# A three-block transformer step on one core: residual and bias adds moved from identity matmuls to VectorE, and a new instruction order

## The chip, the cores and the metric

The kernel runs on one core of a Trainium2 chip. The core has five engines, each with an instruction stream of its own: TensorE (PE) multiplies matrices and writes to PSUM, its weight loads are shown as PEld; VectorE (DVE) works elementwise and reduces along rows; ScalarE (ACT) evaluates functions and copies; GpSimd (POOL) does some small work; SyncE (SP) issues the loads and stores. The streams wait for each other by semaphores only. The metric is the device time of one launch in microseconds (us), the median of several runs. Before the change it is 224.31 us, the median of 3 runs between 224.06 and 224.98.

## The reference

Two rows (batch 2) of 128 tokens with 512 channels go through three residual blocks, each on a layer norm of the row. Everything is float32.

```python
x = x + xattn(layernorm(x), ctx, ...)   # causal self-attention, cross-attention to 2048 context tokens, MLP
x = x + rwkv(layernorm(x), ...)         # the "time" axis is the batch: 2 steps
x = x + moe_attn(layernorm(x), ...)     # attention with expert-mixed values and outputs

# in xattn (single head of 512 channels, scale 1/sqrt(32)):
z = self_attn(x, Wq1, Wk1, Wv1);  x = layer_norm(x + z, ln1_g, ln1_b)
z = cross_attn(x, ctx, Wq2, Wk2, Wv2);  x = layer_norm(x + z, ln2_g, ln2_b)
z = relu(x @ fc1_w + fc1_b) @ fc2_w + fc2_b;  out = layer_norm(x + z, ln3_g, ln3_b)

# end of rwkv:
h = layernorm(inp + (y * g) @ Wo, norm_w, norm_b)
out = layernorm(silu(h @ Wf + bf), lnf_w, lnf_b)

# end of moe_attn: 8 heads of 64, 5 experts, of which 2 are chosen by logits
out = einsum('bthe,bthk,ekd->btd', mask_o, attn, Wo)
```

The self-attention's key count is found from the scores themselves (number of scores of the first query that are not zero), as is that of the cross-attention.

## The kernel before

A row of tokens is a 128 x 512 tile: a token to a partition, the channels along it. Both rows go through the same phases: `queries` (layer norm and Q, K, V of both rows), `self_attention`, `cross_queries`, `cross_attention`, `feed_forward`, `rwkv`, `switch_heads`. For a projection the row is turned (four 128x128 transposes by PE, `turn`) and multiplied with the weights by `project`, mostly in two halves of 256 output channels, each in its own PSUM bank. `matmuls` lists the products of one bank. Where it is given `plus`, it puts one more product in front, the identity `unit` with the row that is to be added: PE adds a residual or a bias into the bank by a matmul.

To be fast, part of the large operands are split into a high and a low half in a reduced float32 format (tiles named hl_; high by an ACT cast, low by a VectorE subtraction) and multiplied in three products; the rest are plain float32 products, which leave two records per matmul in the profile.

The steps of importance here:

- `self_attention` (from line 554): scores, `count`, softmax, the transposed probabilities `pT`, then per half of 256 channels the residual `h` by identity matmul and `pT` times V in the same bank (line 578), moments by `bn_stats` from the bank, and the normalised `x1`.
- `rwkv` (from line 778): after gating, `Y` is turned into `yT`, multiplied with Wo with the residual `inp` as `plus` (line 959), normalised into `hh`, turned, and multiplied with Wf with the bias row `par2[BF]` as `plus` (line 982). ACT takes the tanh of the bank, VectorE forms `f` from tanh and bank.
- `switch_heads` (from line 999): at the end VectorE multiplies the attention output `po` of the even and the odd heads (`par` 0 and 1) with the expert mask into two tiles `me[0]` and `me[1]`. In row 1 the sum over the 8 heads and the transposition are done at once by PE: for each of three pairs of experts eight matmuls with `unit` are summed in a bank (lines 1106 to 1110), four from each tile. Row 0 sums on VectorE and transposes.

The order of work is not that of the program text. Every operation is only recorded (`Program`, `Engine`), and `emit` (line 166) issues the records in the sequence of the string `ORDER`, in which a number is a record and "+2" stands for the two records after it. The sequence is fixed and sets the order on every engine and in the load queue, all by line 169, so all instructions have that line in the profile. Pools give buffers in the order of the records: `stage` (3 buffers of 128 x 512) takes the quarters of weights that are split, `wide` (16) the whole weights, context tiles, rows of parameters and large intermediates. A load waits until the earlier user of its buffer is done, and the loads behind it in the queue wait with it. Eight PSUM banks rotate likewise. `keep_warm` puts a few idle identity matmuls into the stream; `NDUM` and `TAILW` say how many.

Of the kernel before, what the change touches and what calls it, by code (L numbers as in the profile page):

```python
# [42 lines left out]
0 208 1 209+1 215 2 1698 216+1 1718 218 1719 219+1 1699 232 221 1700 8 4 211 3 212 233 222 25 234 20 235+1 214 213 238  # L43
237 228 223+1 26 239 229 21+1 31 244+1 225 246 1720 270 240 247 27 230+1 241 271+3 248 275+2 249 28 34 37 226 23+1
278+1 250+5 280 242 227 256 281 257 243 258+2 282+1 261+3 284+1 265+1 286 29 292 30 32 293+1 287+2 267 35 318 33 295+2
319+1 38 298 36 299+1 321 39 301 322 302+2 323+4 305 328+1 306+1 330+1 5 308+1 332 310+4 333+2 315 40+1 49 43+1 11 19
336 9 337+2 290 268+1 317 340+1 344+1 414 316 415 45 42 346+1 375 12 50 79 46+1 84 376 66 48 291 343 358+1 342 360 377
361 416 51 362 378 348 363 18 379 417 364 87 67 63 418 104 380 419 349 381 365 384 382 56 420 423 350+4 395 366 383
385+1 85 387+2 421+1 424 390 425 69 426 391 6 355 367+1 392 357 396 356 427 393 428 369 429 68 434 371 370 372 397 394
398+3 430 402 373 431+1 435 404+1 433 57 403 436+2 406 1721 407+3 1701 453 463 411 454 10 80 439 455 464 456 465 457  # L50
441 443 466 440 442 447 467 444 468 82 458+2 448 469 74 445 86 88 446 473 483 474 470 450 449 475+2 484+2 478+2 58 64
60+1 471 81 461 481 487+2 493 94 59 62 89 494 490 495+1 462 482 521+2 497 491 65 75 472 524 492 498 525+2 499 528 500
529 109 83 530 501+4 531 97 126 532 374 506 533 77 76 534 507+6 535+1 95 514+2 537+2 98 540 517 541+1 588+1 562 96 518
543+1 563 72 575 564 576 545 78 519 590+2 577 593 565+6 594 578 546 579 70 73 572 549 573 580+1 550 582+1 71 551+2 105
584+1 99 547 106 520 548 92+1 554 586 555+1 595 90 727 596 557 91 558+2 597+1 728 157 599 107 729 102 100 574 108 587
121 127 561 730+2 600 112 733+1 129 735 601+3 101 736+1 618 740+5 738 605 611 606 612 609 746+1 753 748+1 610 607+1
613 54 766+1 754+1 750+1 768+1 615 614 756+2 641 770 623+3 642 771 122 759 103 760 55 643 761 772 616 627 128 773+1
762 775+2 130 644 739 628 123 629 617 630+4 124 635 125 645 137 136 138 763+1 646 752 765 928 636 659 778 660+2 637
140 638+2 779 131 142 663+1 780 647+4 132+1 652+2 781 113+1 134 782 655+1 796 168 657+1 665+1 677 667 135 668 785 783
678 669+2 679 672 787 680 13 15 110 786 784 673+2 789 681 790 676 682+1 619 684 788 791 145 197 792 17 14 794 52 837+2  # L60
7 840 801+1 795 855 803 53 169 139 793 804+1 685 819+1 807 821 856 822 808 857 141 16 111 146 806 809+2 686 812+1 118
143 687 823 814 688 815 689 816+1 692 818 144 825+1 693 824 827+1 858 147 158+1 690 696 829 697 691 830 698+1 831 700
832+2 701 835 841+1 412 115+1 694 702 119 703 413 120 695 117 704+1 150 620 152 706 836 148+1 621 187 622 859 188 151
843+1 707 710 708 711 709 712 845+3 713 163+1 178 849+1 179 714 797 715 451 851+1 165 189 853+1 860+1 716 720+1 153
862 717 723 722 718 180 719 863 904 864 725 905+1 916 866 917 867 907+2 452 865 870+1 868 874 910 875+2 911 170 981
724 869 872 878 154 879 155 880+2 918 160 166 873 883+2 919 161 920+1 913 912 156 914 726 922+1 929+1 798+2 175 931
176 924 167 932 925 162 926 915 933 172 888 886 934+2 889 887 890+2 937 177 938 184 927 893 939+1 894+1 898 199 943
941 896+1 944 942 899+1 969 957 901 173 970 945 958+4 185 963+1 946 966 947+1 971+1 951 949 952 965 950 953+1 973+2
967 955 976+1 956 982 968 983+2 193 902 978 986 1010 987 1011 979 988 1013+1 989+1 1012 991 980 992 1015 1089 1016 993
1017 1099 174 186 181 903 994 1090 996 1020 1067 1022 1069 1108 1018 1107 997 995 998 1091 1024 1140 1092 1073 1109  # L70
1026 1071 1141+1 1139 1028 1100 1029 1075 1093+1 1076 198 1077 1095 1030+1 1101 1070 1021 190 1096 1023 1032 1078 999
182 1033 1102 1116+1 1068 1079 1034 1080 191 196 1001 1004 1000 1025 1005 1035 1002 1006 1003 1007 183 1008 1103 1027
1009 1036 171 1072 1218+1 1081 1037 1221 194 1038 1082 1220 1222 1224+1 1039 1223 1097 195 192 1111 1110 1228 1324
1083 1112+2 1118 1323 1327 1119 1226 1229 1325 1333 1328 1084 1334+1 1326 1085 1336 1045 1329 1040 1074 1086 1343 1231
1279 1098 1282 1307 1346 1330 1280 1308 1232 1281 1233 1283 1046 1305 1344 1230 1234 1044 1306 1115 1047 1284 1286+2
1042+1 1104 1285 1019 1289 1337 1290 1347 1291+1 1235 1293+1 1120 1105 1087 1041 1048 1352 1295 1088 1296 1345 1391
1353 1297 1354+1 1348 1148+1 1392 200 1054 1389 1349+1 1106 1390 1050+1 1309 1150+1 201 1052 1331 1049 1121 1123 1236
1055 1061 1338 1124 1393 1299 1298 1300 1053 1060 1125 1310 1332 1311+1 1237 1122 1356 1339 1127 1238+3 1131 1242+1
1058 1244+1 1301 1341 1059 1246+2 1143 1340 1056 1062 1132 1351 1144 1128 1064 1342 1133 1063 1065 1302 1129 1357 1130
1303 1399 1145+1 1135 1057 1126 1313 1066 1314 1152 1359 1315 1253 1136 1254 1360 1137 1376 1358 1400 1316+3 1256 1252  # L80
1249 204 1250 1170 1401 1134 1251 1255 1138 1153 1257 1264 1258+1 1377 1261 1154 1361 1265 1155 1304 1147 1156 1158+1
1263 1320 1157 1161+1 1164 202 1369 1262 1260 1268 1321 1160 1165 1171 1166 1163 1167 1172 1168 1363 1378 1173+1 1276
1402 1198 1190 1394 1322 1277 1395 207 1373 1278 1379 1273 1267 1270 1269 1374 1380 1382 1362 1272 1371 1375 1274 1169
1396 1364 1271 203 1366 1275 1175 1381 1176 1383 1177 1384 1372 1385+2 1365 1178 1367+1 1388 1180 1179 1370 1266
1181+2 1397 1184 1186 1185 1187+1 1199+2 1189 1202 1191+1 205 1193+1 1403 1398 1203 1404 1406 1405 1407+2 1204 1410+1
1205 1424 1415 1195 1412+2 1416 1418 1417 1419+2 1196+1 1206+3 1212 206 1210 1213 1211 1214+3 1473 1425 1452 1426+2
1422 1472 1475+1 1444 1474 1423 1478+1 1429+2 1477 1481 1480 1432 1487 1482 1434 1433 1436 1435 1227 1437 1483 1440+1
1484 1438+1 1442 1488 1445 1485 1446 1489 1522 1453+2 1523 1447 1443 1513 1456 1448 1511 1486 1457 1524+1 1505 1526+1
1514+1 1490 1516 1496+1 1491+1 1517 1528 1518 1529 1493+1 1498 1519 1499 1520 1506+4 1500 1449 1521 1495 1530 1501
1512 1531 1502+2 1559 1534 1458 1450 1459 1451 1460+3 1466 1464 1467 1465 1468+2 1533 1471 1560+2 1602 1601 1603 1532  # L90
1604 1607+1 1563 1605 1539+2 1606 1567 1542 1564 1536 1610 1609 1543 1565 1611 1566 1535 1612+1 1569 1545 1544 1547
1546 1570 1552 1642 1549 1643 1572+1 1550 1614 1571 1551 1651 1553+1 1652 1537+1 1653 1555 1575 1556 1576 1574 1577
1548 1616 1654 1557+1 1617 1635 1634 1636+1 1568 1644+1 1618+1 1578 1646+1 1620+1 1648 1615 1625 1655 1622 1656 1623
1649 1638 1657 1640 1582 1650 1658 1624 1626+4 1639 1631 1659 1632 1688+1 1633 1579 1641 1663+1 1580 1583 1581 1690+1
1584 1660 1585 1662 1668+2 1586 1692 1671 1696 1587 1661 1588+1 1695 1672 1590 1705 1676 1706 1596 1591 1597 1673+1
1678 1675 1681 1679 1682 1665 1694 1592 1666 1693 1702 1667 1703 1680 1684+1 1683 1686 1677 1712 1687 1707 1697 1704
1708 1713 1709+2 1714 1716+1 1715 1598 1593 1731+1 1722 1733 1740+1 1734 1594 1599 1735 1600 1742 1723+4 1736+1 1743
1728+1 1738 1744+1 1730 1749 1746 1739 1747+1 1595 1754 1750+3 1755+3
"""
OPT = set("""psc fc2 Wv Wk u2col bfpe z4pe z1pe q2 hhcol q2row d3 both1 both4""".split())  # L100

ON_ACT = [set("vsum vc vv bv".split()), set("vsum vc vv bv".split())]
PCR = [{0,1,2},{0,1,2}]
WHOLE = set("Wv1 Wv2 fc2 Wv Wk".split())
VPE = set()
MIX = {"Wq1": 2}
MIXD = set("Ww Wa Wr".split())
CUTW = 2
# [77 lines left out]
def perceiver_kernel(ctx: ExitStack, tc: tile.TileContext, a: dict, out: bass.AP):  # L186
# [46 lines left out]
    for t in range(T):  # L233
        for j in range(2):
            sync.dma_start(X[t][:, half(j)], a["x"][t][:, half(j)])
# [296 lines left out]
    def token(t):  # L532
        return slice(t * P, (t + 1) * P)
# [678 lines left out]
```

## Time and profile before

| | us |
|---|---|
| median of 3 runs | 224.31 (224.06 to 224.98) |
| the profiled execution | 224.74 |
| its span, from first to last instruction | 222.9 |
| PE busy | 215.3, 1246 records |
| VectorE busy | 186.1, 439 records |
| ScalarE busy | 140.2, 400 records |
| GpSimd busy | 17.1, 40 records |
| loads | 43 MB, 195 GB/s on average |
| granted TensorE clock | 0.998 of full speed |

The page cuts the span into 40 slices and gives the busy share of each engine in tenths for every slice. Its chain follows the work that ended last back from the end: at each step to what released the instruction, or to the instruction before it on its engine. A group line gives the shape, the count, then busy time and mean duration, then the idle time of the engine just before such instructions and what ended it. Records of matmuls overlap (a matmul's end is modelled), so that the busy time of PE is no proof that it runs at its peak.

### The profile page before, as it was taken

The numbers are of one execution on the slowest core, as the hardware profiler recorded it, in microseconds if no ns is written. First come the engines' busy times: TensorE is split into PE (matmuls) and PEld (weight loads), VectorE is DVE, ScalarE is ACT, GpSimd is POOL, SyncE is SP. The second block draws the span as 40 slices with busy tenths as digits, with TensorE's granted clock in tenths as the row PEclk, the third lists the DMA queues.
The fourth block names the chain that finished last, engine by engine and source line by source line (L and its number), as shares of the span: only waits on it lengthen the run. The fifth ranks groups of instructions, "written<-read, shape, count | busy, mean of one in ns | idle before, by whom it ended". The sixth has DMA issues, their size and how long they took to land.

```text
span 222.9 us, 3686 instructions
## 1 busy us (share of the span) xinstructions
PE 215.3 (97%) x1246; PEld 182.7 (82%) x1246; DVE 186.1 (83%) x439; ACT 140.2 (63%) x400; POOL 17.1 (8%) x40
## 2 busy tenths in 40 slices
PE   6999999999999999999999999999999999998993
PEld 6999879998778767868788888887886799797892
DVE  4670569998999998989989999999998598999831
ACT  2753569686788998827469889977652614705500
POOL 4200011000000000000111100021213001000000
PEclk9999999999999999999999999999999999999999
DMA  6987799926699999587854999900000000000011
GB/s 157 355 322 255 250 381 386 385 110 238 245 315 354 374 399 375 202 285 209 310 187 102 402 389 387 303 7 0 3 0 0 0 3 1 0 3 0 0 50 47
DMA packets 21897, 43.42 MB, mean 195 GB/s; under 512 B 1283, under 2 KB 2871, under 8 KB 21879
## 3 DMA queue, kind: packets, MB, share of 16 engines
q1 hardware_dynamic: 21879, 43.19, 55.1%
q8 instruction: 10, 0.16, 0.3%
q14 instruction: 8, 0.07, 0.1%
HBM read 42.66 MB, written 0.52 MB: 194 GB/s over the span
## 4 chain that ended last, share of the span: by engine, by line
PE 64%; DVE 24%; DMA 3%; issue 2%; POOL 2%; ACT 2%; SPq 0%; POOLq 0%; DVEq 0%
PE bank L169 64%; DMA w_Wv<-in_Wv_dram 3%; DVE me L169 2%; DVE hl_ctxT L169 2%; DVE Y L169 2%; DVE pr L169 2%; DVE st L169 1%; DVE em L169 1%; DVE hl_ctxN L169 1%; POOL rinv L169 1%; POOL rs L169 1%; DVE ve L169 1%; DVE v L169 1%; DVE u L169 1%; DVE hl_Wv L169 1%
## 5 line engine op out<-in xcount | busy, mean ns | idle before, releaser
L169 POOL TENSOR_TENSOR rinv<-ve,nhalf 128x1 f32<-128x1 f32 x16 | 10.1, 629 | 147.2 <-DVE ve L169 75.4
L169 DVE TENSOR_TENSOR hl_ctxT<-cT,hl_ctxT 128x1024 fp32r<-128x1024 f32 x16 | 19.0, 1216 | 0.8 <-ACT hl_ctxT L169 0.5
L169 PE MATMUL bank<-hl_ctxT,qkTh 128*128 128x512 f32 x64 | 17.8, 395 | 0.1
L169 ACT CAST hl_ctxT<-cT 128x1024 fp32r<-128x1024 f32 x16 | 16.0, 1050 | 2.5 <-PE bank L169 2.5
L169 PE MATMUL bank<-hl_ctxN,pTh 128*128 128x512 f32 x48 | 16.3, 402 | 0.0
L169 DVE TENSOR_TENSOR hl_ctxN<-cN,hl_ctxN 128x1024 fp32r<-128x1024 f32 x12 | 14.4, 1217 | 0.6 <-ACT hl_ctxN L169 0.6
L169 PEld LDWEIGHTS bank<-hl_ctxT,qkTh 128*128 128x128 f32 x64 | 11.7, 188 | 2.8 <-DVE some L169 0.5
L169 DVE TENSOR_TENSOR hl_Wv<-w_Wv,hl_Wv 128x512 fp32r<-128x512 f32 x12 | 8.0, 681 | 6.4 <-ACT hl_Wv L169 6.4
L169 ACT CAST hl_ctxN<-cN 128x1024 fp32r<-128x1024 f32 x12 | 12.3, 1046 | 0.0
L169 PE MATMUL bank<-hl_ctxT,qkTl 128*128 128x512 f32 x32 | 10.4, 396 | 0.0
L169 PEld LDWEIGHTS bank<-hl_ctxN,pTh 128*128 128x128 f32 x48 | 8.9, 189 | 1.6
L169 PE MATMUL bank<-xnT,w_fWk 128*128 128x128 f32 x64 | 10.2, 276 | 0.0
L169 PE MATMUL bank<-hl_ctxN,pTl 128*128 128x512 f32 x24 | 10.1, 421 | 0.0
L169 ACT CAST hl_Wv<-w_Wv 128x512 fp32r<-128x512 f32 x12 | 7.3, 622 | 4.0 <-DMA w_Wv<-in_Wv_dram 3.9
L169 PE MATMUL bank<-xnT,w_fWq 128*128 128x128 f32 x64 | 9.9, 277 | 0.0
L169 PEld LDWEIGHTS bank<-u2T,w_fc 128*128 128x128 f32 x64 | 8.2, 191 | 1.4 <-ACT u2T L169 1.1
L169 PEld LDWEIGHTS bank<-xnT,w_fWq 128*128 128x128 f32 x64 | 8.6, 192 | 0.7 <-ACT xnT L169 0.3
L169 PEld LDWEIGHTS bank<-xnT,w_fWk 128*128 128x128 f32 x64 | 8.9, 192 | 0.2
L169 PE MATMUL bank<-u2T,w_fc 128*128 128x128 f32 x64 | 8.5, 278 | 0.3 <-ACT u2T L169 0.3
L169 PE MATMUL bank<-w_Wa,mix 128*128 128x256 f32 x32 | 8.7, 379 | 0.0
L169 PE MATMUL bank<-unit 128*128 128x128 f32 x32 | 6.9, 391 | 1.7 <-POOL unit masks.py:199 1.7
L169 PE MATMUL bank<-w_Wr,mix 128*128 128x256 f32 x32 | 8.4, 379 | 0.0
(289 smaller groups left out, 614.8 us busy)
## 6 DMA issues: line engine op xcount, KB each, us to landing
cT<-in_ctxT_dram SPq DMA_DIRECT2D x8, 1024.0 KB, 6.7
cN<-in_ctx_dram SPq DMA_DIRECT2D x8, 1024.0 KB, 7.5
spread<-in_spread_dram SPq DMA_DIRECT2D x9, 512.0 KB, 8.5
w_Wv<-in_Wv_dram SPq DMA_DIRECT2D x12, 256.0 KB, 5.3
w_Wk<-in_Wk_dram SPq DMA_DIRECT2D x8, 256.0 KB, 5.3
w_Wq<-in_Wq_dram SPq DMA_DIRECT2D x4, 256.0 KB, 4.5
w_Wk2T<-in_Wk2T_dram SPq DMA_DIRECT2D x4, 256.0 KB, 6.9
w_Wq<-in_Wq_dram SPq DMA_DIRECT2D x1, 1024.0 KB
```

The source lines that it names most:

```text
L169: self.tc.keep_in_program_order(op(*args, **kwargs))
```

## The change

Four things are done by VectorE that PE did by identity matmuls, and the order is new.

- First attention, both rows (`z1d`): no `plus`; VectorE adds `h` to the bank into the half of `x1`, and moments and normalisation read `x1` instead of the bank.
- Wo, both rows (`Z4D`): no `plus`; VectorE adds `inp` to the bank into the half of `hh`, and moments and normalisation read `hh`.
- Wf, row 1 only (`BFD`): the path without `plus`, which was in the code: VectorE adds the bias into `f`, ACT takes the tanh of `f`, VectorE forms the product from `f`.
- Head sums, row 1 (`me2`): before the matmuls of a pair of experts VectorE adds the pair of `me[1]` onto that of `me[0]`, and PE sums four products instead of eight.
- `ORDER` is another sequence throughout, for the loads too.

The options `xact`, `u1back` and `pow1` come into the text but are not switched on.

```diff
-0 208 1 209+1 215 2 1698 216+1 1718 218 1719 219+1 1699 232 221 1700 8 4 211 3 212 233 222 25 234 20 235+1 214 213 238
...
+215+3 0 208 1718+1 219+2 1 209+1 1720+1 222 2 232 211 3 21 233 4 234+1 20 212 236 213 22 214 223+1 228 225 229 237
...
-OPT = set("""psc fc2 Wv Wk u2col bfpe z4pe z1pe q2 hhcol q2row d3 both1 both4""".split())
+OPT = set("""psc me2 z1d fc2 Wv Wk u2col bfpe z4pe z1pe q2 hhcol q2row d3 both1 both4""".split())
...
+Z4D, BFD = {0, 1}, {1}
...
             for j in range(2):
                 pz = bank([P, C // 2])
-                matmuls(pz, [(pT[:, :P], V[t][:, half(j)])], True, h[t][:, half(j)])
-                dve.bn_stats(m.st[:, j, :], pz)
-                zs.append(pz)
+                if "z1d" in OPT:
+                    matmuls(pz, [(pT[:, :P], V[t][:, half(j)])], True)
+                    z = x1[:, half(j)]
+                    dve.tensor_add(z, pz, h[t][:, half(j)])
+                else:
...
+                dve.bn_stats(m.st[:, j, :], z)
+                zs.append(z)
...
+        hh = row("hh")
         m = Moments()
         if "z4pe" in OPT:
             zs = []
-            for j, c, po in project(yT, W["Wo"], plus=inp):
+            for j, c, po in project(yT, W["Wo"], plus=None if t in Z4D else inp):
+                if t in Z4D:
+                    zz = hh[:, c]
+                    dve.tensor_add(zz, po, inp[:, c])
+                    po = zz
                 dve.bn_stats(m.st[:, j, :], po)
                 zs.append(po)
...
-        if "bfpe" in OPT:
+        if "bfpe" in OPT and t not in BFD:
             for j, c, po in project(hhT, W["Wf"], plus=par2[BF]):
...
             for c, e in enumerate((0, 2, 3)):
                 pt = bank([P, P])
                 keep_warm(0 if c else TAILW[2], pt)
-                matmuls(pt, [(m[:, i, e : e + 2, :].rearrange("p e d -> p (e d)"), unit) for m in me for i in range(4)], True)
+                if "me2" in OPT:
+                    n = pairs[c]
+                    dve.tensor_add(me[0][:, :, n], me[0][:, :, n], me[1][:, :, n])
+                ms = me[:1] if "me2" in OPT else me
+                matmuls(pt, [(m[:, i, e : e + 2, :].rearrange("p e d -> p (e d)"), unit) for m in ms for i in range(4)], True)
                 act.copy(aT[:, c, :], pt)
```

## The prediction

> **What bounds the kernel now.** The page first: engine shares, slices, chain.
>
> ```profile
> span 222.9 us, 3686 instructions
> ...
> PE 215.3 (97%) x1246; PEld 182.7 (82%) x1246; DVE 186.1 (83%) x439; ACT 140.2 (63%) x400; POOL 17.1 (8%) x40
> ...
> PE   6999999999999999999999999999999999998993
> ...
> DVE  4670569998999998989989999999998598999831
> ...
> PE 64%; DVE 24%; DMA 3%; issue 2%; POOL 2%; ACT 2%; SPq 0%; POOLq 0%; DVEq 0%
> ```
>
> TensorE (PE) is busy nearly everywhere, but VectorE (DVE) is close behind from a sixth of the span on. So an engine's share over the span settles nothing; I cut the span where the chain that ended last changes its engine, and asked for busy time in these stretches.
>
> ```profile
> 18.00:33.11 15.11, 15.11 (x88) 12.60 (x88) 7.01 (x31) 8.75 (x23) 0.64 (x2) 1.00 0.85 307
> 33.11:41.45 8.34, 8.34 (x75) 8.27 (x74) 7.93 (x17) 6.46 (x13) 0.87 (x7) 1.00 1.05 385
> 41.45:112.94 71.49, 70.36 (x356) 55.56 (x355) 67.08 (x131) 53.12 (x94) 1.49 (x2) 1.00 0.83 291
> 112.94:143.60 30.66, 30.66 (x157) 26.45 (x158) 29.78 (x82) 27.24 (x99) 2.35 (x4) 1.00 0.84 296
> 143.60:172.08 28.48, 27.85 (x131) 22.86 (x129) 26.92 (x79) 17.43 (x85) 5.91 (x6) 1.00 0.03 11
> 172.08:192.89 20.81, 20.81 (x128) 16.95 (x129) 16.86 (x42) 10.16 (x36) 2.07 (x3) 1.00 0.00 1
> 192.89:204.64 11.75, 11.75 (x107) 11.44 (x105) 11.41 (x22) 3.34 (x11) 0.00 (x0) 1.00 0.01 1
> ...
> 209.67:219.89 10.22, 9.77 (x72) 8.88 (x71) 4.70 (x9) 0.76 (x3) 0.00 (x0) 1.00 0.08 27
> ```
>
> After length come PE, PEld, DVE, ACT, POOL, then clock, DMA share, GB/s. VectorE has room in the first attention (7.01 of 15.11) and in the tail (4.70 of 10.22). Between 33.11 and 172.08 it has 131.7 of 139.0 us: two engines are full at once, and in 143.6 to 172.1 the chain runs over VectorE (pr, Y, st, f, X, xn, one behind the other) while PE is at 98%. The prices come from the groups by shape and from the timeline:
>
> ```profile
> L169 PE MATMUL bank<-unit,me 128*128 128x128 f32 x48 | 5.7, 276 | 0.0
> ...
> L169 PE MATMUL bank<-h,unit 128*128 128x256 f32 x8 | 2.5, 392 | 0.0
> L169 PE MATMUL bank<-inp,unit 128*128 128x256 f32 x8 | 2.4, 380 | 0.0
> L169 PE MATMUL bank<-spread,unit 128*128 128x256 f32 x8 | 2.2, 379 | 0.0
> ```
>
> ```profile
> 151.35 1.89 PE L169 MATMUL bank<-w_Ww,mix 128*128 128x256 f32 x8
> 211.29 5.11 PE L169 MATMUL bank<-unit,me 128*128 128x128 f32 x44
> 212.88 0.75 DVE L169 TENSOR_TENSOR res<-bank,X 128x256 f32<-128x256 f32 x2
> ```
>
> **The change, part by part.** A float32 matmul leaves two records that overlap their neighbours, so the mean of one is no price. Eight records of 128x256 take 1.89 us: (1.89 - 0.38)/7 = 0.216 a record, 0.43 us a matmul. For 128x128, (5.11 - 0.28)/43 = 0.112, 0.225 us a matmul. Gone are four h,unit, four inp,unit, two of the four spread,unit and twelve of the 24 unit,me matmuls: 10 x 0.43 + 12 x 0.225 = 7.0 us of PE. New on VectorE: ten adds of 128x256 (0.42 each, 0.33 where another follows: 0.75 - 0.42), two of 128x512 (0.69 or 0.60, from the ve products, 1.29 for two) and one more of 256: 10 x 0.33 + 2 x 0.60 + 0.33 = 4.8 us. ACT's count stays at 342 instructions. The edits and the order work together, so I go by stretch.
>
> *First attention (18 to 33).* PE sheds 4 x 0.43 = 1.7, but the chain scores, count, exp, V matmul, moments, x1 then has no filler left. Before, the last score of row 0 is followed by its count at 24.55, 3.85 after the first Wv1 matmul at 20.70; the new order puts six Wv1 matmuls (0.23) and five scores (0.225) there, 2.5 us, so the chain starts 1.35 earlier. It grows by two adds in front of the moments, 0.7. I take -0.65; PE waits about 1 us in that chain. Bounds: -1.7 (PE full) and +0.7 (the start gains nothing). Row 1's chain has row 0's Wq2 matmuls as cover; without it, its own two adds would cost 0.7, within the bound. The scheme needs the second cT load sooner: SyncE now issues two cT before the fourth Wv1 quarter, which waits for a stage buffer anyway (issued 14.88 before).
>
> *The middle (33 to 172).* From the two instruction orders, with a duration for each from the trace: VectorE's work from the first x1 to row 0's xn was 130.3 us and is 128.6. Two low halves of ctxT (1.2 each) move ahead of the softmax of the first attention, into idle time; row 0's two Wo adds (0.7) and the bias add into row 1's X (0.6) come in front of xn; the rest are shifts. PE loses four Wo identities and one Wf identity there, 5 x 0.43 = 2.15. At the share it has now (0.948), VectorE needs 128.6/0.948 = 135.7, 1.8 less by its own count. Both engines allow about the same: -1.9. Bounds: -2.15, and +1.3, if the early ctxT halves buy nothing (0.7 + 0.6 stay).
>
> *Loads.* ACT's casts of Wv quarters waited 3.9 us for DMA, and the chain has 6.95 us of that load just before 108.9; PE then waits 0.3 at 110 and 0.3 at 113. The new SyncE order issues one Wv quarter among the cT loads, all eight cN in a row and fc1 at PE's 77th us of work instead of at 95.1 us. I take the two waits as gone: -0.6; bounds 0 and -1.2, twice that, for the waits that ride on them. Wg, Wo and Wf move behind fcat, fWk and fWq: by buffer releases they leave at about 120, 125 and 136 and are used at 147, 156 and 161. With 2.5 MB ahead at 300 GB/s (8 us) they still land first; without that cover a late Wf costs what it is late. POOL's order changes by nothing on the chain.
>
> *Row 1 after 172.* PE loses 0.43 (the other Wf identity). Row 1's chain gets two Wo adds (0.7, during PE's fcat and fWq of row 0) and two Wf adds in front of the tanh, 0.42 not covered, since the q/k matmuls left behind Wf last 5.4 + 1.6 and the chain there took 7.1. Tanh sits behind these adds on ACT with only evacuations queued after it. Net 0, bounds -0.4 and +0.7. The 192.9 to 204.6 stretch is VectorE's, 11.41 of 11.75, with the same instructions in slightly other order: 0, bounds -0.6 and +0.6 (one ve product).
>
> *Tail.* From the first me product of row 1 (209.67) PE ends 9.8 us later. Now: product 1.40, product of the first pair 0.69, its add 0.69 and a hand-over 0.1: PE starts the pair's four matmuls at +2.9 instead of +1.6. Pair two and three follow VectorE (0.6 + 0.6, then 0.4 + 0.45): the last four matmuls begin at +5.05 and end at +5.95; six fWo matmuls of 0.43 make +8.55. Gain 1.2, where PE alone would give 2.7. Bounds -2.7 and +0.3 (three adds uncovered, 1.8, less half of 2.7 with waits).
>
> Sum: -0.65 - 1.9 - 0.6 + 0 - 1.2 = -4.35. Against the profiled execution, 224.74 (span 222.9 and 1.8 around it), 220.4; this execution stood 0.4 over the median of 224.31, so **220.0**.
>
> [...]
>
> **Rivals.**
>
> (1) PE alone binds. For it: its waits for others sum to only 4.0 us. Against: the chain in 143 to 172. All 7.0 come back: 217.3.
>
> (2) VectorE binds the middle, and what comes off PE there is idle time. For it: 0.948 busy. The middle then costs +1.3 rather than -1.9, the rest stays: 224.31 - 2.45 + 1.3 = 223.2.
>
> (3) Slower: one load is late. The fourth quarter of Wv2 is now issued only when the Wv quarter's low half has freed its stage buffer, at VectorE's work 67.9, and is wanted there at 73.7, 5.8 us later (before, it left at 77.97 and was wanted 14 us later). A quarter lands after 5.3 us (median of the Wv loads), the cast takes 0.62: margin -0.1. VectorE stands in order behind it, and PE behind VectorE, so each us late is a us lost. For it: the DMA share is 0.9 to 1.05 there. Against: cN leaves earlier, so the queue is shorter. It decides over 5.5 us late (landing after 11 us, as fcat and fWk did at 15.7): 225.5 to 227.
>
> That the order does not do what it says is excluded: PE's and VectorE's instruction counts change by -22 and +13.
>
> **How the numbers follow.** The forecast (218.3 to 222.2) 0.48, (1) 0.15, (2) 0.21, (3) 0.16. A measurement of this kernel tells about 0.5% from no change (223.2 to 225.4). Faster: 0.48 + 0.15 + half of (2), 0.73; same: the other half, 0.11; slower 0.16. The range runs from 216.6, under (1), to 225.5, which leaves out most of (3).
>
> **What would show it.** PE busy down by 6 to 7 us, VectorE up by about 5; row 0's x1 transposes near 32.4, xn of row 0 near 169, the unit,me matmuls in three groups of four that each wait for DVE me; ACT's hl_Wv idle under 2 us. Wrong if xn comes at 172 or later (the middle did not shrink), or if the waits list shows PE or DVE behind w_Wv.

## The result: slower by 1.1 per cent, with TensorE at half its clock in the tail

The changed kernel takes 227.18 us, the median of 12 executions between 225.54 and 228.40; the kernel before, measured beside it, 224.70 us (223.89 to 225.60, 12 executions). The ratio is 1.0106, with a 95% interval from 1.008 to 1.0131. The forecast was 220.0, with a range up to 225.5, so it missed in sign and in range. The profiled execution took 226.15 us, one of the better ones: span 223.5 and 2.65 around it.

The page of the changed kernel first, the lines that answer to those shown of before, and the row of the granted clock:

```profile
span 223.5 us, 3617 instructions
...
PE 212.6 (95%) x1202; PEld 178.7 (80%) x1202; DVE 189.8 (85%) x452; ACT 140.0 (63%) x400; POOL 17.7 (8%) x40
...
PE   6999999999899999999999999999997998996994
...
DVE  3568588988999899989899999999997599999461
...
PEclk9999999999999999999999999999999999999589
...
PE 64%; DVE 21%; ACT 6%; DMA 3%; issue 3%; POOL 2%; POOLq 0%; ACTq 0%; DVEq 0%
```

TensorE's busy time fell by 2.7 us only, although 22 matmuls worth 7.0 are gone, and the clock row says why: in before it reads 9 throughout, here it ends in 5, 8, 9. The stretches of the prediction, cut near the same places of this trace (columns as before: length, PE, PEld, DVE, ACT, POOL, clock, DMA share, GB/s):

```profile
18.00:32.00 14.00, 13.83 (x82) 11.38 (x81) 9.94 (x37) 9.14 (x26) 0.55 (x1) 1.00 0.93 324
...
143.00:171.06 28.06, 26.33 (x122) 21.34 (x121) 26.81 (x80) 18.02 (x82) 5.46 (x6) 1.00 0.01 1
171.06:191.50 20.44, 19.77 (x124) 16.27 (x125) 16.57 (x42) 8.65 (x29) 2.07 (x3) 1.00 0.00 1
191.50:203.55 12.05, 11.72 (x105) 11.18 (x103) 11.96 (x24) 4.35 (x18) 0.00 (x0) 1.00 0.00 1
203.55:209.22 5.67, 4.05 (x21) 3.27 (x21) 3.87 (x10) 4.49 (x21) 0.00 (x0) 0.82 0.00 0
209.22:220.90 11.68, 11.20 (x56) 9.78 (x55) 6.43 (x11) 0.70 (x3) 0.00 (x0) 0.79 0.10 34
```

Up to 203.55 the clock is whole, and the kernel stood 1.1 us better than before at the same event (the exponentials of row 1: 204.67 there). The tail then loses more than that. In shorter windows it is plain what comes ahead of the fall:

```profile
199.60:203.00 3.40, 3.37 (x33) 3.15 (x32) 3.40 (x6) 0.94 (x3) 0.00 (x0) 1.00 0.00 0
203.00:206.40 3.40, 1.48 (x8) 0.72 (x7) 3.37 (x6) 2.85 (x17) 0.00 (x0) 1.00 0.00 0
206.40:209.80 3.40, 3.40 (x20) 3.18 (x19) 1.63 (x5) 1.64 (x6) 0.00 (x0) 0.62 0.00 0
209.80:213.20 3.40, 3.40 (x12) 2.95 (x12) 2.30 (x4) 0.00 (x0) 0.00 (x0) 0.50 0.00 0
213.20:216.60 3.40, 3.40 (x22) 3.09 (x22) 2.71 (x6) 0.00 (x0) 0.00 (x0) 0.88 0.01 5
```

From 203.0 to 206.4 TensorE is busy for 1.48 of 3.40 us; from about 207.2 to 214.0 the clock stands at 0.50. TensorE's timeline there:

```profile
201.52 1.72 PE L168 MATMUL bank<-kT,qT 64*128 64x128 f32 x16
204.06 1.03 PE L168 MATMUL bank<-ident,es 128*128 128x128 f32 x3 [0.82 <-ACT es L168]
206.16 0.44 PE L168 MATMUL bank<-ident,es 128*128 128x128 f32 x2 [1.07 <-ACT es L168]
206.43 0.27 PE L168 MATMUL bank<-ident,me 128*128 128x128 f32 x1
206.54 0.29 PE L168 MATMUL bank<-ident,es 128*128 128x128 f32 x1
206.67 0.27 PE L168 MATMUL bank<-ident,me 128*128 128x128 f32 x1
206.78 0.38 PE L168 MATMUL bank<-ident,es 128*128 128x128 f32 x2
207.00 0.27 PE L168 MATMUL bank<-ident,me 128*128 128x128 f32 x1
207.24 3.22 PE L168 MATMUL bank<-v,eT 128*128 128x64 f32 x14
...
211.53 3.62 PE L168 MATMUL bank<-w_fWo,aT 128*128 128x256 f32 x10
214.99 2.84 PE L168 MATMUL bank<-unit,me 128*128 128x128 f32 x24
```

From the end of the q/k products (kT,qT) at 203.24 to the first v,eT at 207.24 TensorE runs transpositions alone (`ident`, one record each; a plain float32 product leaves two). The fourteen records of v,eT, 3.22 us here, would take about 1.75 (the experiments show it), the ten of fWo 3.62 instead of 2.4. Why TensorE was empty is in the order, not in the edits. In before, row 0's aT was copied in between row 1's exponentials on ScalarE (at 205.37), and four of row 0's six fWo products, eight records, ran in the shadow of these exponentials. Of before:

```profile
205.53 0.44 PE L169 MATMUL bank<-ident,es 128*128 128x128 f32 x2 [0.68 <-ACT es L169]
205.90 1.56 PE L169 MATMUL bank<-w_fWo,aT 128*128 128x256 f32 x6
...
207.81 0.60 PE L169 MATMUL bank<-w_fWo,aT 128*128 128x256 f32 x2
```

In the new order the copy stands on ScalarE behind the last eT of row 1, and the six products behind all but one of row 1's attention products. TensorE was left to wait for the exponentials: 0.82 and 1.07 us in one piece, and some smaller holes.

### The profile page after: what moved, and what is told of

Same layout as the page of the kernel before. It is cut to its first block, busy times and chain, and to the rows that moved or that the text cites. A ratio compares the mean times of both kernels' runs of the same rounds, so it can differ in the third digit from the quotient of the medians.

```text
span 223.5 us, 3617 instructions
## 1 busy us (share of the span) xinstructions
PE 212.6 (95%) x1202; PEld 178.7 (80%) x1202; DVE 189.8 (85%) x452; ACT 140.0 (63%) x400; POOL 17.7 (8%) x40
## 4 chain that ended last, share of the span: by engine, by line
PE 64%; DVE 21%; ACT 6%; DMA 3%; issue 3%; POOL 2%; POOLq 0%; ACTq 0%; DVEq 0%
PE bank L168 64%; DMA cN<-in_ctx_dram 3%; DVE ve L168 3%; DVE me L168 2%; DVE em L168 2%; DVE hl_ctxT L168 2%; DVE st L168 2%; POOL rinv L168 2%; ACT hl_ctxT L168 1%; DVE X L168 1%; ACT es L168 1%; DVE f L168 1%; ACT em L168 1%; ACT hl_ctxN L168 1%; DVE gt L168 1%
## 5 line engine op out<-in xcount | busy, mean ns | idle before, releaser
L168 POOL TENSOR_TENSOR rinv<-ve,nhalf 128x1 f32<-128x1 f32 x16 | 10.6, 663 | 148.0 <-DVE ve L168 145.7
L168 PE MATMUL bank<-hl_ctxT,qkTh 128*128 128x512 f32 x64 | 18.9, 400 | 0.0
L168 DVE TENSOR_TENSOR me<-bank,mo 128x1280 f32<-128x1280 f32 (+2 forms) x6 | 6.2, 1041 | 2.8 <-PE bank L168 2.8
L168 PE MATMUL bank<-w_Wf,hhT 128*128 128x256 f32 x32 | 7.9, 384 | 0.1
```

Of the source, the lines that this page charges most:

```text
L168: self.tc.keep_in_program_order(op(*args, **kwargs))
```

## Experiments

The theory, called C in what follows: the loss is the granted clock, which fell because TensorE was too empty for some 3 us. Its rival, V: the adds on VectorE and the longer chain make the tail longer by themselves. Sequences below are pieces of the order string; records 1668 to 1671 and 1688 to 1691 are row 1's q/k products, 1693 to 1696 and 1673 to 1676 its exponentials, 1702 to 1706 and 1678 to 1682 their transpositions (1680 and 1704 copy them to eT), 1587 to 1589 the transpositions of row 0's head sums, 1590 the copy of aT, 1591 to 1593 and 1596 to 1598 row 0's fWo products.

All runs, each against the kernel before in the same round:

| run | median us (executions) | ratio to before, 95% interval | clock |
|---|---|---|---|
| the change | 227.18 (12) | 1.0106, 1.0080 to 1.0131 | 0.985 or 0.977 |
| + nine idle matmuls (e1) | 222.76 (4) | 0.9918, 0.9888 to 0.9948 | 1.00 |
| the same again (e10) | 222.88 (6) | 0.9895, 0.9868 to 0.9922 | 1.00 |
| + four idle matmuls (e12) | 222.99 (6) | 0.9907, 0.9883 to 0.9931 | 1.00 |
| + row 0's products in the gap (e2) | 223.34 (4) | 0.9938, 0.9917 to 0.9958 | 1.00 |
| before, with the gap (e3) | 230.38 (4) | 1.0244, 1.0209 to 1.0280 | 0.985 or 0.978 |
| edits in the old order (e4) | 234.63 (4) | 1.0446, 1.0419 to 1.0472 | 0.985 or 0.978 |
| new order, no edit, idle matmuls (e5) | 227.92 (6) | 1.0138, 1.0106 to 1.0170 | 1.00 |
| e1 without the edit of the first attention (e6) | 224.34 (12) | 0.9972, 0.9951 to 0.9993 | 1.00 |
| e1 without the edit of Wo (e7) | 223.65 (12) | 0.9956, 0.9932 to 0.9980 | 1.00 |
| e1 without the edit of Wf (e8) | 223.95 (12) | 0.9963, 0.9939 to 0.9986 | 1.00 |
| e1 without the edit of the head sums (e9) | 225.47 (12) | 1.0027, 1.0007 to 1.0046 | 1.00 |
| e1 with one more GpSimd instruction (e11) | 223.08 (8) | 0.9911, 0.9881 to 0.9942 | 1.00 |

### Idle matmuls in the gap

```diff
     def keep_warm(n, o):
...
                 keep_warm(TAILW[par] if t and j == 0 else 0, pt[:, 0, :])
+                if t and j == 0:
+                    idle.append(pt[:, 0, :])
...
+    keep_warm(5, idle[0])
+    keep_warm(4, idle[1])
     program.emit(ORDER)
...
-1670+1 1586 1702 1705 1703 1672
+1670+1 1755+3 1586 1702 1705 1703 1750+4 1672
```

> The changed kernel, with nine identity matmuls more whose results are never read: four behind the last q/k product of row 1, five between the third and the fourth transposition of its exponentials. They fill places where TensorE stood empty (0.8 and 1.1 us between 203.0 and 206.2). Theory C (the granted clock fell to 0.5 from 207.4 to 214.0 because TensorE ran almost empty before, and the slow matmuls delay the second me product from about 209.9 to 211.8): the clock stays at 1.00 in 207 to 214, the last matmul comes about 2 us earlier, and the median goes from 227.2 to 223.5 to 224.5, with less spread. Theory V (the adds of the head sums on VectorE, and the rest of the new order, make the tail longer by themselves): TensorE was only waiting there, so 227.2 stays, or 227.5 with the added matmuls, whatever the clock does.

Measured: 222.76 us, 0.9918 of before, clock 1.00; repeated in a later round 222.88 and 0.9895. That is 4.3 us less than the changed kernel, for nine matmuls *more*, and better than the kernel before. Of this run, TensorE's timeline:

```profile
202.91 1.16 PE L168 MATMUL bank<-unit 128*128 128x128 f32 x8
...
204.66 1.28 PE L168 MATMUL bank<-unit 128*128 128x128 f32 x10
...
206.97 1.75 PE L168 MATMUL bank<-v,eT 128*128 128x64 f32 x14
...
209.21 2.38 PE L168 MATMUL bank<-w_fWo,aT 128*128 128x256 f32 x10
211.43 2.91 PE L168 MATMUL bank<-unit,me 128*128 128x128 f32 x24
```

The groups "bank<-unit" are the idle matmuls. The fourteen records of v,eT now take 1.75 us, the ten of fWo 2.38, and the head sums start at 211.43 instead of 214.99. Theory V falls: VectorE's adds are all still there. C's price was 2.7 to 3.7 us; it was 4.3. The profiled executions differ by 3.5, about what 6.83 us at half clock cost a TensorE that is full (an estimate: half of it, 3.4); five of the twelve executions of the change have a lower mean clock than the profiled one.

> The kernel with nine idle matmuls once more, unchanged, as the base of this round, in five rounds. Its first four executions gave 222.76 (222.28 to 223.66) and 0.9918 of the kernel before; if that was no luck of four, 222.5 to 223.3 and a ratio of 0.990 to 0.995. If it was, it lies by the runs with one edit undone, 223.6 to 224.

Measured: 222.88 us, within the range, and 0.9895, a little under it. The first four executions were no luck.

### Half as many

```diff
-1670+1 1586 1702 1705 1703 1672
+1670+1 1750+3 1586 1702 1705 1703 1672
```

> The changed kernel with only the first four of the nine idle matmuls, 0.9 us, behind the last q/k product of row 1; the hole of 1.1 us between the third and the fourth transposition stays. It asks how much emptiness the clock forgives. In the run with row 0's products in the gap TensorE was empty for 0.8 us of 203 to 205 and full again behind, and the clock stayed at 1.00. If it goes by the share of some us, not by the longest hole, the clock stays up here too and the time is the base's. If a hole of 1.1 us is enough, it falls as in the changed kernel: about 227, clock 0.98.

Measured: 222.99 us, 0.9907, clock 1.00. Four idle matmuls, 0.9 us, are as good as nine, with the 1.07 us hole left as it is:

```profile
203.00:206.40 3.40, 2.31 (x16) 1.61 (x15) 3.40 (x6) 2.71 (x16) 0.00 (x0) 1.00 0.00 0
206.40:209.00 2.60, 2.60 (x23) 2.37 (x23) 1.66 (x6) 1.78 (x7) 0.00 (x0) 1.00 0.00 0
```

2.31 busy of 3.40 us kept the clock, 1.48 lost it, with a hole of the same 1.07 us in both, so that this hole alone did not decide it. The idle matmuls are products, not transpositions, and the run doesn't tell whether their busy time or their kind made the difference (last section).

### Real work in the gap

```diff
-1693 1695 1694 1696 1670+1 1586 1702 1705 1703 1672
+1693 1695 1694 1670+1 1586+4 1696 1702 1705 1703 1596 1591 1597 1672
...
-1679 1587 1681 1588 1682 1704
+1679 1681+1 1592 1704
```

> The changed kernel with real work in the same gap: the three transpositions of row 0's head sums, the copy of aT and four of its six Wo products move ahead of the transpositions of row 1's exponentials, about where the kernel before has them. Theory C: as with idle matmuls, the clock stays up, and since the four products (1.7 us) no longer stand between the attention products and the head sums, 223 to 224. Theory V: 226.5 to 227.5, since the chain of VectorE behind the first me product (1.40 + 0.69 + five more) is as long as it was.

Measured: 223.34 us, 0.9938, clock 1.00, with TensorE busy 2.53 of the 3.40 us from 203.0. That is C again. It is not better than idle matmuls: row 1's first me product starts at 208.7 instead of 208.1, since transpositions now wait behind fWo products, and the head sums wait for VectorE with nothing to fill in. This run also has a second place, an emptier window with a hole of 1.19 us in it, in which the clock held:

```profile
209.60:213.00 3.40, 2.11 (x13) 1.49 (x13) 3.33 (x6) 0.00 (x0) 0.00 (x0) 1.00 0.00 0
```

### The same gap in the kernel before

```diff
-1692 1671 1696 1587 1661 1588+1 1695 1672 1590 1705 1676 1706 1596 1591 1597 1673+1
+1692 1671 1696 1661 1695 1672 1705 1676 1706 1673+1
...
-1679 1682 1665 1694 1592 1666
+1679 1682 1665 1694 1666
...
-1680 1684+1
+1680 1587+2 1684+1
...
-1704 1708 1713 1709+2 1714
+1704 1590 1708 1713 1709+2 1596 1591 1597 1592 1714
```

> The kernel before, with the opposite move: transpositions of row 0's head sums, the copy of aT and the first four Wo products go behind the transpositions and attention products of row 1, so that TensorE has about 3 us with little work at 204 to 207. No edit of the change is in it. Theory C: the granted clock falls to about 0.5 for several us behind 208, the mean to about 0.98, and 226.5 to 228. Theory V: the same matmuls in another order, 224 to 225.5, clock near 1.00.

Measured: 230.38 us, 1.0244, clock 0.985 (one execution 0.978). No edit is in it: the place of eight records in the tail costs the kernel before 5.9 us.

```profile
205.40:208.80 3.40, 1.27 (x6) 0.65 (x6) 3.33 (x6) 2.87 (x16) 0.00 (x0) 1.00 0.00 0
```

```profile
209.00:211.00 2.00, 2.00 (x11) 2.00 (x12) 0.64 (x4) 1.51 (x5) 0.00 (x0) 0.58 0.00 0
211.00:213.00 2.00, 2.00 (x12) 2.00 (x11) 1.29 (x1) 0.00 (x0) 0.00 (x0) 0.50 0.00 0
...
215.00:217.00 2.00, 2.00 (x8) 1.71 (x7) 0.04 (x1) 0.00 (x0) 0.00 (x0) 0.72 0.00 0
```

The first row is a window ahead of the fall, with 1.27 of 3.40 us busy, the others are the clock behind it. C gave 226.5 to 228 for this; it was underpriced, because the four fWo products also cost their own time once they stand in the tail, where TensorE is full (all twelve records of row 0's fWo take 4.28 us there, partly at half clock). An estimate: half of 6.83 us at half clock and 1.7 us for four products make 5.1; the profiled executions differ by 6.0, and what makes the rest was not traced.

### What the edits are worth

First all four in the old order: the sequence of before, each add directly before what reads it, and only row 1's head sums in the tail as in the new order.

```diff
-OPT = set("""psc fc2 Wv Wk u2col bfpe z4pe z1pe q2 hhcol q2row d3 both1 both4""".split())
+OPT = set("""psc me2 z1d fc2 Wv Wk u2col bfpe z4pe z1pe q2 hhcol q2row d3 both1 both4""".split())
+Z4D, BFD = {0, 1}, {1}
```

> All four edits of the change in the order of the kernel before: its sequence, the identity matmuls dropped, each add put directly before what reads it, and only the head sums of row 1 in the tail as in the new order. Loads and row 0's Wo products stand as before, so the gap is filled. If the edits are worth what the prediction's steps gave them without the new order (TensorE relieved by 7.0 us, VectorE loaded by 4.8), 220 to 223 and the clock near 1.00. If VectorE binds and the adds come on top, 225 to 228 with the clock still near 1.00.

Measured: 234.63 us, 1.0446, clock 0.985 or 0.978. I had expected the clock near 1.00. Of this run's VectorE, and then of its TensorE (start, duration, and in brackets the idle time ahead of it and what ended it):

```profile
183.63 0.42 DVE L169 TENSOR_TENSOR f<-bank,spread 128x256 f32<-128x256 f32 x1 [5.57 <-PE bank L169]
183.97 0.56 DVE L169 TENSOR_TENSOR gt<-gl 128x400 bf16<-128x400 f32 x1
...
186.59 0.42 DVE L169 TENSOR_TENSOR f<-bank,spread 128x256 f32<-128x256 f32 x1
```

```profile
189.76 1.25 PE L169 MATMUL bank<-kT,qT 64*128 64x128 f32 x8
194.59 0.33 PE L169 MATMUL bank<-ident,xn 128*128 128x128 f32 x1 [3.58 <-DVE xn L169]
```

```profile
191.00:195.00 4.00, 0.34 (x2) 0.14 (x1) 3.44 (x11) 0.30 (x1) 0.94 (x2) 1.00 0.01 2
...
197.00:199.00 2.00, 2.00 (x7) 1.46 (x7) 0.70 (x2) 1.35 (x8) 0.00 (x0) 0.50 0.00 0
```

VectorE stands 5.57 us at the first bias add of Wf, waiting for the bank, and the comparisons of row 0's gates, which ran in just this time before, stand in order behind it. They follow at 183.97, and the second add comes at 186.59. Row 1's xn is 6.4 us later than before, TensorE is empty for 3.58 us, and the clock falls there too. The time, 234.6, is far outside both of the expected ranges. So the edits need an order other than this one; the loss of the new order is made elsewhere.

Then the reverse, with the idle matmuls as base: the new order without any edit, and without one edit each. Where an edit is undone, identity matmuls stand directly before the products of their bank.

```diff
-OPT = set("""psc me2 z1d fc2 Wv Wk u2col bfpe z4pe z1pe q2 hhcol q2row d3 both1 both4""".split())
+OPT = set("""psc fc2 Wv Wk u2col bfpe z4pe z1pe q2 hhcol q2row d3 both1 both4""".split())
...
-Z4D, BFD = {0, 1}, {1}
+Z4D, BFD = set(), set()
```

> None of the four edits: all residuals, biases and head sums by identity matmuls as before, but in the new order, with the nine idle matmuls in the gap so that the clock stays up (base: the run with idle matmuls, 222.8 against 224.5 for the kernel before). It tells what the edits are worth in the order that was made for them. If TensorE binds in the new order, its 22 matmuls come back in full: 7.0 us, 229 to 230. If VectorE binds between 33 and 172 us (rival 2 of the prediction), TensorE's matmuls stand partly in idle time while VectorE sheds 4.8 us: 223 to 226. If the order alone makes the gain: 222 or less.

Measured: 1.0138 of before, against 0.9907 for the base (the mean of its two rounds): the edits are worth 2.3 per cent, 5.2 us, once the order is the new one and the clock is up. The median of 227.9 lies between the two ranges that were expected, which fits neither engine binding alone. And the new order without the edits is 3 us slower than the old one. In the profiled execution, the fastest of the six, it is 2.1: up to the first me product it costs nothing (209.69 in this run, 209.67 in before); 1.7 us are lost from there to the last add, and 0.4 behind it. What the median has beyond that was not traced.

```profile
210.82 2.38 PE L168 MATMUL bank<-w_fWo,aT 128*128 128x256 f32 x10
213.03 5.52 PE L168 MATMUL bank<-unit,me 128*128 128x128 f32 x48
218.39 2.76 PE L168 MATMUL bank<-w_fWo,aT 128*128 128x256 f32 x12
```

Row 0's fWo products lie in the tail, and TensorE is full from there to the end. In before, four of them (1.7 us) had been done in the gap.

```diff
-OPT = set("""psc me2 z1d fc2
+OPT = set("""psc me2 fc2
```

> The base with idle matmuls, one edit undone: the residual of the first attention comes from identity matmuls again (four of 0.43 us on TensorE, four adds fewer on VectorE in front of the moments). If TensorE is full there, 1.7 us slower than the base. The prediction gave the first attention 0.65 of gain in all, most of it from the order: then within 0.5 of the base. What is left of the edits' 5.1 us (order alone 227.9 against 222.8) after the other three (0.9, 1.2 and 2.7) is 0.3.

Measured: 0.9972 against 0.9895 for the base in the same round, 1.7 us, as much as its four identity matmuls take. In the profiled executions it is 1.1: row 0's x1 transpositions start at 32.7 instead of 31.7, and that difference is carried to the end. I had expected at most 0.5.

```diff
-Z4D, BFD = {0, 1}, {1}
+Z4D, BFD = set(), {1}
```

> The base with idle matmuls, one edit undone: the residual of Wo comes from identity matmuls again in both rows (four matmuls of 0.43 us on TensorE, four adds of 0.33 to 0.42 fewer on VectorE). If TensorE binds: 1.7 us slower than the base, 224.5. If the chain over VectorE binds in these stretches: 0.7 to 1.4 us faster, 221.4 to 222.1. Half and half: within 0.5 of 222.8.

Measured: 0.9956, 1.1 us over the base (0.5 in the profiled executions). That is less than the 1.7 us of TensorE that the edit takes away, and the trace has the rest. From 164 to 170 us, base first, then this run:

```profile
164.00:170.00 6.00, 4.74 (x22) 3.36 (x20) 5.05 (x17) 1.04 (x3) 1.20 (x2) 1.00 0.00 0
```

```profile
164.00:170.00 6.00, 5.96 (x28) 4.38 (x26) 5.19 (x16) 1.04 (x3) 1.10 (x2) 1.00 0.00 0
```

With the identity matmuls TensorE is full in these 6 us; without them it waits 1.26 us: 0.47 in front of row 1's Wo for ScalarE's yT, and the rest behind it for VectorE, which makes row 0's xn (0.87 in all, 0.43 with the identity matmuls).

```diff
-Z4D, BFD = {0, 1}, {1}
+Z4D, BFD = {0, 1}, set()
```

> The base with idle matmuls, one edit undone: the bias of row 1's Wf comes from identity matmuls again (two of 0.43 us on TensorE), tanh reads the bank directly, and two adds leave the chain from the last Wf product to the row's X. The prediction put 0.42 us of them uncovered on the way from 172 to 192. If so, 0.4 to 0.8 us faster than the base, 222.0 to 222.4; if TensorE binds there, 0.9 slower, 223.7.

Measured: 0.9963, nominally 1.3 us over the base, though two identity matmuls make 0.86. In the traces row 1's xn transpositions differ by 0.3 us and the last add by 0.2, so I don't take this size as real; in the profiled execution 4.2 us lie behind the last add instead of 2.7, and the edit touches nothing there. That undoing it does not gain 0.4 to 0.8 is clear.

```diff
-OPT = set("""psc me2 z1d fc2
+OPT = set("""psc z1d fc2
```

> The base with idle matmuls, one edit undone: the head sums of row 1 use all 24 products again (twelve more of 0.225 us on TensorE), without the three adds on VectorE. The prediction gave the tail 1.2 us of gain from this edit, and at most 2.7. If that holds, 224.0 (up to 225.5); if the three adds cost what the matmuls save, 222.8.

Measured: 1.0027, 2.7 us over the base: twelve matmuls of 0.225 us, in full. Both runs start the me products at 208.1 to 208.2; the head sums then take 5.52 us of TensorE instead of 2.91.

By the intervals of their ratios, each of these four differences is uncertain by some 0.7 us. By the last add of the profiled executions they are 1.1, 0.5, 0.2 and 2.7 us, 4.5 in sum, and 4.2 for all four edits at once.

### Time outside the span

```diff
+    pool.memset(nhalf, -0.5)
     program.emit(ORDER)
```

> The base with one instruction more on GpSimd, a memset of 0.1 us at 1.7 us that repeats the one before it. All kernels in the order of before have 70 instructions on GpSimd and 1.8 to 1.9 us of their time outside the span; all in the new order have 69 and 2.5 to 2.6. If that difference hangs on how many instructions GpSimd has to fetch, the time outside the span falls to 1.8 to 1.9 and the time by about 0.4 us (the wait inside the span at its very end, 0.41 in the kernel before, comes back). If it hangs on the order in another way, 2.5 to 2.6 stays.

Measured: 223.08 us, 0.9911, no gain. All executions but one have 2.13 to 2.39 us outside the span, neither 1.85 nor 2.55, and a wait of 0.41 us on GpSimd at the end of the span that the base doesn't have. From the end of the last store's issue to the end of the execution it is 4.8 to 4.9 us with and without the memset, and 4.5 in before. So with one more GpSimd instruction 0.2 to 0.4 us of it lie inside the span instead of outside (the base has 2.55 to 2.58 outside, one execution aside), and the sum is the same. What makes the 0.4 us stays open.

## Why the prediction was wrong

**The step that failed is the tail, with the gap in front of it.** The prediction's stretches end at 204.64 and begin again at 209.67. The 5 us between them, in which four of row 0's fWo products ran while row 1's exponentials were made, have no term, and the stretch ahead of them has "the same instructions in slightly other order: 0". The new order took these products out of the only gap and put them into the tail, and the emptied gap cost 4.3 us of clock. The prediction costed every hole of TensorE at its own length and nothing else, and the tail in prices taken at a clock of 0.998. None of the rivals had this mechanism.

For the tail it said that from the first me product of row 1 TensorE would end 8.55 us later, -1.2 against before. In the changed kernel it took 11.2 (209.22 to 220.42). With the clock up, in the base, it took 8.8 (208.09 to 216.93). That this is near 8.55 is luck, because the path was another one. The sum lets the head sums wait for VectorE three times. In the base TensorE does not wait at all from the first me product to its end: row 0's fWo products stand in front of the head sums. The edit of the head sums is then worth its full 2.7 us where the sum gave it 1.2, and the products moved into the tail, 1.7 us in the run without edits, take most of that back. With four of these products in the gap again (e2) the head sums do wait for VectorE; they start 2.96 us behind the first me product, where the prediction had 2.9, and the tail takes 8.85 (208.68 to 217.53). The two paths happen to be equally long. (In the tail's upper bound, 1.8 less half of 2.7 is 0.45 and not 0.3; nothing rests on it.)

Stretch by stretch, between the same events in the profiled executions, in us against before:

| | predicted | changed kernel | with the clock up (e10) |
|---|---|---|---|
| to row 0's x1 | -0.65 | -1.7 | -1.4 |
| from there to row 0's xn (middle and loads) | -2.5 | 0.0 | -0.6 |
| to row 1's xn | 0 | +1.0 | +1.0 |
| to the first me product of row 1 | 0 | +0.3 | -0.6 |
| to the last add | -1.2 | +1.4 | -0.9 |
| behind the last add | 0 | +0.4 | +0.4 |
| sum | -4.35 | +1.4 | -2.1 |

The median lies 1.0 us above the profiled execution: seven of the twelve executions have a mean clock of 0.985 and a median of 226.2, five have 0.977 and 227.8.

**First attention.** Right in sign, too small. Its sum let VectorE's chain eat most of the gain; undoing the edit alone costs 1.7 us by the medians, the bound given for a full TensorE, and 1.1 by the profiles.

**The middle and row 1.** Too large by 1.9 and 1.0. The share at which VectorE could be used (0.948) was taken for a capacity, which left out where the waits would stand. From the end of row 1's Wo to its hh transpositions before took 3.0 us and the base takes 4.7: row 1's two adds and its moments stand behind row 0's chain on VectorE, and TensorE stands still for 0.87 us at row 0's xn. By the profiles 1.2 of the 1.7 us that Wo's edit took off TensorE came back; 0.9 of them are the waits for yT and xn that the identity matmuls had filled. This is what rival 2 described, in one place instead of the whole stretch. The 130.3 and 128.6 us of VectorE's work that I compared are sums over the stretch and say nothing of its end.

**Loads.** The waits of the Wv casts for DMA, 3.9 us before, are gone as forecast (none in the list of waits), but casts of cN (2.7 us) and w_fc (3.1 instead of 1.1) wait instead, and the chain runs over a load of cN for 3% of the span as it did over a load of Wv before. The waits have moved rather than gone. Rival 3 did not occur: nothing waits for w_Wv.

**VectorE or TensorE.** The prediction priced TensorE's matmuls as in a full run (0.216 us a record of 128x256). Undoing single edits bears this out in part. By the medians 1.7 of 1.7 (first attention), 1.1 of 1.7 (Wo), 1.3 of 0.9 (Wf) and 2.7 of 2.7 us (head sums) of matmuls come back, each uncertain by 0.7, and 5.2 of 7.0 for all. By the profiles TensorE is full in the tail (2.7), mostly in the first attention (1.1) and hardly at Wo (0.5).

**What would show it.** TensorE's busy time was to fall by 6 to 7 us: 2.7, which was the visible trace of the clock. VectorE's was to rise by about 5: 3.7. Row 0's x1 was to come near 32.4 (31.4) and xn near 169 (170.3). The head sums were to wait three times for VectorE: they ran in one piece from 214.99, because TensorE was by then behind VectorE, and in one piece from 211.43 in the base too.

## What to carry to other kernels

Where work leaves TensorE, look at what is left for it in the gaps it has to wait out, not only at the sum. A stretch of 4.0 us in which TensorE ran some transpositions and nothing else cost 4.3 us by the half clock behind it, and 0.9 us of idle matmuls bought that back; the kernel before, with such a gap of 4.63 us and no edit, lost the clock too (0.50 for 6.8 us). Read the clock row of the profile before any duration is compared, and put a new wait on an in-order engine only behind the work that can run meanwhile (the 5.57 us of the edits in the old order). An edit and the order made for it are to be priced apart: here the edits gained 5.2 us, the order lost 3 of them, and the clock cost 4.3, more than was left.

## What the runs showed of the hardware

The traces record two levels of the clock, 1.00 and 0.50. In the change 201.39 us at 1.00 are recorded ahead of the fall, then 6.83 at 0.50 and 10.24 at 1.00. In three profiles the clock fell while there were matmuls left, and the low stretch was about 6.8 us long in each: 207.2 to 214.0 in the change, 209.3 to 216.1 in e3, 195.2 to 202.0 in e4. It began 4.0 to 4.2 us behind the end of the last product ahead of it. In before it fell behind the work only, at 222.15, 2.7 us after the last matmul. The executions of the change have two mean clocks, 0.985 and 0.977; an estimate from them and the two levels: 0.985 of 223.5 us is 6.7 us at half clock, 0.977 of 225.8 is 10.4.

What emptiness loses the clock these runs leave open. In the windows of 3.40 us TensorE was busy for 1.48 us in the change (from 203.0), 1.27 in e3 (from 205.4) and 0.01 in e4 (from 191.0), and the clock fell behind them; it was busy for 2.31 in e12 (from 203.0) and 2.11 in e2 (from 209.6), and the clock held. The kind of work differs too: in the three that lost it, all that TensorE did between the last product and the next was transpositions. It went without a product for 4.00 us in the change (203.24 to 207.24), 4.63 in e3 (205.24 to 209.87) and 5.18 in e4 (191.01 to 196.19); in e12, which kept the clock, for 2.91 us at this place (204.48 to 207.39). No run filled the gap with transpositions alone, which would tell busy time and kind of work apart.
